# Scores on all 64 partitions of a head: a change to the row count of two products in a one-core decoder layer

## The chip, the cores and the metric

The kernel runs on one core of one Trainium2 chip, as one launch. The metric is device time in microseconds (us), the median of the runs. Three runs of the kernel before gave 5751.36 us as median, from 5746.47 to 5760.46.

## What is computed

A decoder layer in float32, for 8 sequences of 512 tokens with 512 channels. A selective state-space block (1024 inner channels, 16 states), then cross attention with a context of 512 tokens, then a mixture of experts with one shared expert; a layer norm over the sum with its input follows each. The part that the change touches is the attention, 16 heads of 32 channels. Cut to what matters:

```python
qm = split_heads(q @ Wq.T + bq)          # 8 x 16 heads x 512 x 32
km = split_heads(k @ Wk.T + bk)
scores = einsum('bnlh,bnph->bnlp', qm, km) / sqrt(32)
scores = where(mask, scores, -1e8)
attn = softmax(scores, axis=-1)
out = einsum('bnlp,bnph->bnlh', attn, vm)
```

## The kernel before, in words

Three stages follow one another: `layers` (state-space block, attention, shared expert and routing), `experts` (32 experts, each on 640 slots) and `finish` (the last layer norm).

**The layers.** The state-space block works in 16 chunks of 256 tokens, two for each sequence. A chunk has 32 steps (4 pairs of 128 channels, 4 groups of states, 2 halves). In a step VectorE does a product (L441), a scan along time (L445) and a second product (L462), ScalarE the decays before it (L429), and TensorE sums states into `py` (L466). The B and C rows of a step are spread over partitions by copies on SyncE's queue (SP): `bcast`, L373, issued one group of states ahead of their use.

**Units beside the scan.** What comes after the state-space block of sequence b - 1 is cut into some 160 units (`units`), each a TensorE part and what takes its result. The main loop hands them out between the steps of sequence b's two chunks, as many as a written weight allows (`own`, `spent`, `whole`), so TensorE, VectorE and ScalarE take scan and attention work in program order, mixed. The last sequence's units have no scan beside them and run one after another.

**The scores.** Heads go in pairs, 8 pairs to a sequence. Each pair has a buffer `qa` and a buffer `ka` of 128 partitions x 512 tokens, of three each that take turns (`NPB` = 3, L198 to L205). The first head has partitions 0 to 63, the second 64 to 127. Within a head's 64 partitions:

- 0 to 31: queries (`qa`) or keys (`ka`), copied in by `spread` (L717, L718);
- 32: ones in `qa`, the mask's fill value (0 or -1e8) in `ka` (L719);
- 33: minus the largest score of each query in `qa`, put there later by `negate` (L745); ones in `ka`;
- 34 to 63: ones in both, set once at the start, and not read.

`maximum` (L729) takes the product over partitions 0 to 32, 33 rows, for 128 queries by 512 keys, both heads into one tile `ps_s`; VectorE reduces it (L731). `negate` transposes the four columns of maxima of a pair (L738), ScalarE turns the sign (L742), and two copies on SP put the rows into `qa`. `weigh` (L755) then takes the product over partitions 0 to 33, 34 rows, for 128 keys by 512 queries, so that the maximum is taken off within the product; ScalarE takes the exponential (L759). `gather` (L771) multiplies by the values, with a block of ones beside them that gives the sums.

**The order.** In the list of units, step n (n from 0, four to a pair) adds the spread of pair i + 2 when pair i begins, then `maximum` for step n + 6, with `negate` two steps after a pair's last maximum, then `weigh` for step n and `gather` for step n - 1. All copies named go by SP's queue in that order, with `bcast`, weights and the copies of results (L791, L792) between them. A spread waits for the `weigh` that read its buffers three pairs before.

**Setup.** At the start SP issues some 30 small copies of constants; the mask's copy, the weights and the first tokens (`load_x`, L266) stand behind them. GpSimd sets constants at the same time.

Of the kernel before, what the change touches and what calls it, by code (L numbers as in the profile page):

```python
# [16 lines left out]
P = 128  # L17
B, S, D = 8, 512, 512
DC = D // P
# [14 lines left out]
HD = 32  # L34
# [47 lines left out]
def layers(ctx, tc, a, x1d, filld, based, xbuf):  # L82
# [20 lines left out]
    nc = tc.nc  # L103
# [66 lines left out]
    ones = cp.tile([P, P], F32, name="l_ones")  # L170
# [28 lines left out]
    qas, kas = [], []  # L199
    for i in range(NPB):  # L200
        qas.append(cp.tile([P, S], F32, name=f"l_qa{i}"))
        kas.append(cp.tile([P, S], F32, name=f"l_ka{i}"))
        for t in (qas[i], kas[i]):
            for r0 in (HD, 2 * HD + HD):
                nc.gpsimd.memset(t[r0 : r0 + HD], 1.0)  # L205
    va = cp.tile([P, SC, NH // 2, 3 * HD], F32, name="l_va")
    nc.gpsimd.memset(va[:, :, :, HD : 2 * HD], 1.0)

# [435 lines left out]
    def units(b):  # L644
# [66 lines left out]
        def spread(i):  # L711

            n = (b * NH // 2 + i) % NPB
            st[i] = qa, ka = qas[n], kas[n]
            for j in range(2):
                r0, r1 = (i % 2) * 2 * HD + j * HD, j * 2 * HD
                nc.sync.dma_start(qa[r1 : r1 + HD, :], st["qT"][r0 : r0 + HD, i // 2, :])  # L717
                nc.sync.dma_start(ka[r1 : r1 + HD, :], st["kT"][r0 : r0 + HD, i // 2, :])  # L718
                nc.sync.dma_start(ka[r1 + HD : r1 + HD + 1, :], filld[b : b + 1, :])  # L719

        def maximum(i, lt):

            qa, ka = st[i]
            if lt == 0:
                st["mx", i] = p2.tile([P, SC, 2], F32, tag="mx", name="mx")
            ps = pss.tile([P, 2, S], F32, tag="sc", name="ps_s")
            for j in range(2):
                r = slice(j * 2 * HD, j * 2 * HD + HD + 1)
                nc.tensor.matmul(ps[:, j, :], qa[r, lt * P : (lt + 1) * P], ka[r, :], start=True, stop=True)  # L729
            mx = st["mx", i]  # L730
            return lambda: nc.vector.tensor_reduce(mx[:, lt, :].unsqueeze(2), ps, AX.X, ALU.max) and None  # L731
# [17 lines left out]
        def weigh(i, kc):  # L749

            qa, ka = st[i]
            ps = pss.tile([P, 2, S], F32, tag="sc", name="ps_t")
            for j in range(2):
                r = slice(j * 2 * HD, j * 2 * HD + HD + 2)
                nc.tensor.matmul(ps[:, j, :], ka[r, kc * P : (kc + 1) * P], qa[r, :], start=True, stop=True)  # L755

            def exponentials():
                st["eT", i, kc] = eT = p2.tile([P, 2, S], F32, tag="eT", name="eT")
                nc.scalar.activation(eT, ps, AF.Exp)  # L759

            return exponentials
# [116 lines left out]
        for j in range(DC):  # L878
            add(3.4, queries, j, dry=(j == 0))
        add(0, spread, 0)  # L880
        add(0, spread, 1)
        pairs, ahead = NH // 2, SC + 2
        late = []

        def max_at(m):

            if late:
                add(0.4, negate, late.pop(), dry=True)
            if m < pairs * SC:
                add(0.9, maximum, m // SC, m % SC)  # L890
                if m % SC == SC - 1:
                    late.append(m // SC)
# [4 lines left out]
        for n in range(pairs * SC + 4):  # L897
            i, k = n // SC, n % SC
            if k == 0 and i + 2 < pairs:
                add(0, spread, i + 2)  # L900
            max_at(n + ahead)
            if i < pairs:
                add(0.9, weigh, i, k)
            if 0 < n <= pairs * SC:
                add(0.9, gather, (n - 1) // SC, (n - 1) % SC)

            if n > 3 and (n - 3) % (2 * SC) == 0:
                add(0, divide, (n - 3) // (2 * SC) - 1, dry=(n > pairs * SC))
# [78 lines left out]
    for i, (b, t) in enumerate(chunks):  # L987
        nf = {}
        after = chunks[i + 1] if i + 1 < len(chunks) else None
        if t == 0 and b:  # L990
            side, spent = units(b - 1), 0.0

            own = [work(k) for k in range(len(steps))] * 2
            whole = sum(own) + sum(x[0] for x in side)
# [71 lines left out]
    for _, fn, alone in units(B - 1):  # L1066
        do(fn, first=alone)
# [198 lines left out]
def program(tc, a, out):  # L1266
    nc = tc.nc
    with tc.tile_pool(name="dram", bufs=1, space=DRAM) as dram:
        x1d = dram.tile([N, D], F32, name="x1d")
        filld = dram.tile([B, S], F32, name="filld")  # L1270

        based = dram.tile([N + P, D], F32, name="based")
        xbuf = dram.tile([SLOTS, ROW], F32, name="xbuf")
        nc.scalar.preload_act_table_set(LN_EXP)

        with ExitStack() as ctx:
            layers(ctx, tc, a, x1d, filld, based, xbuf)
        with ExitStack() as ctx:
            experts(ctx, tc, a, xbuf, based)
        with ExitStack() as ctx:  # L1280
            finish(ctx, tc, based, out)
# [31 lines left out]
```

## Time and profile before

| what | value |
|---|---|
| median of three runs | 5751.36 us |
| lowest and highest | 5746.47 and 5760.46 us |
| the profiled execution's own time | 5761.86 us |
| its span, first to last instruction | 5760.2 us |
| mean granted TensorE clock | 0.907 |
| TensorE busy, weight loads apart | 5098.1 us |
| VectorE busy | 4111.1 us |
| ScalarE busy | 2554.4 us |
| the layers, up to about | 4080 us |

How to read the lines that the prediction shows. The page gives the busy time of each engine (PE is TensorE's matmul, PEld its weight load, DVE VectorE, ACT ScalarE, POOL GpSimd, SP SyncE's queue), with the span in 40 slices of 144 us below it; a digit of PEclk is the clock that TensorE was granted in that slice, in tenths. A group of instructions has line, engine and operation, what is written from what, the shape, the count; then busy time in all, mean ns of one; then the engine's idle time just before them, and what ended most of it. "33*128 33x512" is a product over 33 rows with 128 stationary columns and 512 streamed ones. A float32 product has two records, and a busy PE is not PE at its peak, as ends are modelled. The table of stretches gives, for each part of the span, its length, each engine's busy time with the count of records, the mean granted clock, the share of the DMA engines and GB/s. A line of waits names who waited, for whom, us in all, times, and the longest.

### The profile page before, as it was taken

How to read it: one execution, taken by the hardware profiler on the slowest of the kernel's cores; microseconds unless marked ns; L12 is line 12 of the kernel's file. 1: busy time of each engine (PE TensorE's matmuls, PEld its weight loads, DVE VectorE, ACT ScalarE, POOL GpSimd, SP SyncE). 2: the span in 40 equal slices, each digit the busy share in tenths (PEclk: the TensorE clock that was granted, in tenths of full speed). 3: DMA queues.
4: the chain of work that ended last, by engine and by line, in shares of the span. 5: the costliest groups of instructions: out<-in, count | busy, mean ns of one | idle time of the engine just before them, and what ended most of it. 6: DMA issues, size and time to landing. Idle time of an engine off the chain costs nothing. (4 is left out here: it accounts for less than half of the span.)

```text
span 5760.2 us, 57381 instructions
## 1 busy us (share of the span) xinstructions
PE 5098.1 (89%) x18984; PEld 2615.0 (45%) x18984; DVE 4111.1 (71%) x5290; ACT 2554.4 (44%) x5347; POOL 514.7 (9%) x424
## 2 busy tenths in 40 slices
PE   5658989888988898989898899889899999999994
PEld 3324344344434433434443443342466666666662
DVE  5998889888889888988988898843444444444443
ACT  4555564554655556455455545523122222222223
POOL 0000001002000100100100020010111111111111
PEclk8779889899889988988988897998999999999997
DMA  7685345335434533533543362431444444444444
GB/s 206 194 230 170 88 120 164 107 112 171 119 107 119 178 95 113 164 105 110 158 131 103 101 192 73 116 123 36 145 119 116 121 115 119 121 122 115 114 122 135
DMA packets 480489, 744.19 MB, mean 129 GB/s; under 512 B 64050, under 2 KB 196666, under 8 KB 480192
## 3 DMA queue, kind: packets, MB, share of 16 engines
q1 hardware_dynamic: 442688, 655.24, 38.0%
q0 software_dynamic: 33280, 76.90, 7.0%
q10 hardware_dynamic: 4224, 8.39, 0.4%
q8 instruction: 150, 2.46, 0.2%
q14 instruction: 147, 1.20, 0.1%
HBM read 491.91 MB, written 148.28 MB: 111 GB/s over the span
## 5 line engine op out<-in xcount | busy, mean ns | idle before, releaser
L429 ACT ACTIVATE l_da<-both,l_aneg 128x256 f32<-128x256 f32 x2048 | 893.6, 499 | 811.0 <-DVE h L445 753.5
L445 DVE TENSOR_TENSOR_SCAN h<-l_da,h 128x1028 f32<-128x1028 f32 x512 | 1170.9, 2292 | 72.7 <-ACT h L435 49.3
L466 PE MATMUL py<-h,l_twice 128*64 128x256 f32 x4096 | 666.4, 438 | 213.6 <-DVE h L462 213.5
L441 DVE TENSOR_TENSOR h<-both,bc 128x1024 f32<-128x1024 f32 x512 | 618.5, 1214 | 167.9 <-PE py L466 108.8
L462 DVE TENSOR_TENSOR h<-h,bc 128x1024 f32<-128x1024 f32 x512 | 622.8, 1218 | 6.0
L466 PEld LDWEIGHTS py<-h,l_twice 128*64 128x64 f32 x4096 | 309.2, 153 | 607.2 <-issue 258.3
L1212 PE MATMUL po<-w,hT 128*128 128x512 f32 x1280 | 575.1, 592 | 0.0
L729 PE MATMUL ps_s<-l_ka,l_qa 33*128 33x512 f32 x1024 | 347.1, 766 | 114.8 <-DVE mx L731 114.4
L1146 PE MATMUL ps_h<-xT,w 128*128 128x320 f32 x1536 | 435.7, 433 | 0.0
L731 DVE TENSOR_REDUCE mx<-ps_s 128x2 f32<-128x1024 f32 x256 | 310.5, 1216 | 115.1 <-PE ps_s L729 114.6
L1167 DVE TENSOR_TENSOR hT<-ps_h,p 128x320 f32<-128x320 f32 x128 | 62.9, 491 | 443.8 <-PE ps_h L1146 443.8
L1217 POOL DMA_INDIRECT based<-y,xe x160 | 251.1, 1569 | 1359.4 <-ACT y L1216 856.6
L1216 ACT ACTIVATE y<-po,xe 128x512 f32<-128x512 f32 x160 | 110.0, 687 | 551.6 <-PE po L1212 542.6
L1146 PEld LDWEIGHTS ps_h<-xT,w 128*128 128x128 f32 x1536 | 292.4, 190 | 131.7 <-issue 15.6
L755 PE MATMUL ps_t<-l_qa,l_ka 34*128 34x512 f32 x1024 | 339.8, 740 | 10.7 <-ACT eT L759 10.3
L771 PE MATMUL po<-eT,l_va 128*64 128x512 f32 x1024 | 322.0, 712 | 16.2 <-ACT raw L783 11.1
L759 ACT ACTIVATE eT<-ps_t 128x1024 f32<-128x1024 f32 x256 | 258.9, 1014 | 174.5 <-PE ps_t L755 174.0
L1212 PEld LDWEIGHTS po<-w,hT 128*128 128x128 f32 x1280 | 231.1, 190 | 231.6 <-issue 224.1
L1146 PE MATMUL ps_h<-t,s 128*128 128x320 f32 x1024 | 286.2, 432 | 0.0
L677 PE MATMUL ps_p<-x2T,wa 128*128 128x512 f32 x512 | 251.1, 642 | 18.2 <-DVE hT L846 16.2
L495 PE MATMUL po<-wm,zs 128*128 128x512 f32 x512 | 245.5, 632 | 22.3 <-DMA wm<-in_out_proj_w 16.8
L297 PE MATMUL ps_x<-xnT,wm 128*128 128x256 f32 x1024 | 255.3, 405 | 4.9 <-ACT dt L395 3.6
(205 smaller groups left out, 6711.3 us busy)
## 6 DMA issues: line engine op xcount, KB each, us to landing
bc<-scr SPq DMA_DIRECT2D x1024, 128.0 KB
w<-in_w SPq DMA_DIRECT2D x96, 1024.0 KB
wm<-in_in_proj_w SPq DMA_DIRECT2D x128, 512.0 KB
xbuf<-zero SPq DMA_DIRECT2D x32, 1362.5 KB
xe<-xbuf SPq DMA_DIRECT2D x32, 1362.5 KB
both<-dt SPq DMA_DIRECT2D x256, 128.0 KB
both<-dtx SPq DMA_DIRECT2D x256, 128.0 KB
wm<-in_out_proj_w SPq DMA_DIRECT2D x64, 512.0 KB
```

The source lines that it names most:

```text
L429: nc.scalar.activation(da[:, n, 1:], dt[:, c % 2, j, :], AF.Exp, scale=aneg[:, c, j, g, m : m + 1])
L441: nc.vector.tensor_tensor(steps, dtx[:, c % 2].unsqueeze(2).to_broadcast([P, 2, NG // 2, T]), bc[0], ALU.mult)
L445: nc.vector.tensor_tensor_scan(flat, da.rearrange("p n t -> p (n t)"), flat, 0.0, ALU.mult, ALU.add)
L462: nc.vector.tensor_tensor(steps, steps, bc[1], ALU.mult)
L466: nc.tensor.matmul(py[j * HP : (j + 1) * HP, c % 2, :], twice, h[:, j * 2 + m, 1:], start=False, stop=(s == (NST // NG - 1, NG // 2 - 1, 1)),)
L729: nc.tensor.matmul(ps[:, j, :], qa[r, lt * P : (lt + 1) * P], ka[r, :], start=True, stop=True)
L731: return lambda: nc.vector.tensor_reduce(mx[:, lt, :].unsqueeze(2), ps, AX.X, ALU.max) and None
L755: nc.tensor.matmul(ps[:, j, :], ka[r, kc * P : (kc + 1) * P], qa[r, :], start=True, stop=True)
L759: nc.scalar.activation(eT, ps, AF.Exp)
L771: nc.tensor.matmul(po[j * 2 * HD : (j + 1) * 2 * HD, :], va[:, kc, i, j * HD : (j + 2) * HD], eT[:, j, :], start=(kc == 0), stop=(kc == SC ...
L1146: nc.tensor.matmul(ps, w[:, n, r * P : (r + 1) * P], x[:, n, :], start=not more and n == 0, stop=n == 1, skip_group_check=more,)
L1212: nc.tensor.matmul(po, got["hT"][:, ic, j * P : (j + 1) * P], got["w2"][:, ic, :], start=(ic == 0), stop=(ic == DC - 1))
```

## The change

The two products go over all 64 partitions of a head, in place of 33 and 34. So that the 30 further rows add nothing, `ka` holds zeros from partition 32 of each head on at the start, and ones in partition 33 alone, which six copies on SP put there at setup[...]. `qa` keeps its ones. Since `maximum` now reads partition 33 too, where `qa` still holds the maxima of three pairs before, `spread` clears that row by one more copy for each head, from a row of zeros of `ka`: two a pair, 128 in all.

```diff
@@ layers, buffers
         for t in (qas[i], kas[i]):
             for r0 in (HD, 2 * HD + HD):
-                nc.gpsimd.memset(t[r0 : r0 + HD], 1.0)
+                nc.gpsimd.memset(t[r0 : r0 + HD], 1.0 if t is qas[i] else 0.0)
+        for r0 in (HD + 1, 2 * HD + HD + 1):
+            nc.sync.dma_start(
+                kas[i][r0 : r0 + 1, :].rearrange("p (c t) -> p c t", c=DC),
+                ones[0:1, :].unsqueeze(1).to_broadcast([1, DC, P]),
+            )
@@ spread
                 nc.sync.dma_start(ka[r1 + HD : r1 + HD + 1, :], filld[b : b + 1, :])
+                nc.sync.dma_start(qa[r1 + HD + 1 : r1 + HD + 2, :], ka[r1 + HD + 2 : r1 + HD + 3, :])
@@ maximum
-                r = slice(j * 2 * HD, j * 2 * HD + HD + 1)
+                r = slice(j * 2 * HD, (j + 1) * 2 * HD)
                 nc.tensor.matmul(ps[:, j, :], qa[r, lt * P : (lt + 1) * P], ka[r, :], start=True, stop=True)
@@ weigh
-                r = slice(j * 2 * HD, j * 2 * HD + HD + 2)
+                r = slice(j * 2 * HD, (j + 1) * 2 * HD)
                 nc.tensor.matmul(ps[:, j, :], ka[r, kc * P : (kc + 1) * P], qa[r, :], start=True, stop=True)
```

## The prediction

> **What bounds the kernel now.** I read the page first, then the busy time of each engine by stretches, then the waits. The page:
>
> ```profile
> span 5760.2 us, 57381 instructions
> ...
> PE 5098.1 (89%) x18984; PEld 2615.0 (45%) x18984; DVE 4111.1 (71%) x5290; ACT 2554.4 (44%) x5347; POOL 514.7 (9%) x424
> ...
> PEclk8779889899889988988988897998999999999997
> ...
> L729 PE MATMUL ps_s<-l_ka,l_qa 33*128 33x512 f32 x1024 | 347.1, 766 | 114.8 <-DVE mx L731 114.4
> L755 PE MATMUL ps_t<-l_qa,l_ka 34*128 34x512 f32 x1024 | 339.8, 740 | 10.7 <-ACT eT L759 10.3
> ```
>
> To be seen: TensorE is busiest, and in the layers (slices 1 to 28) it often has less than its full clock; the two products that change hold 687 us of it. The layers' own bound is read from the scores' stages, the stretch of each batch from its first L729 to its last L771 (the eighth has no scan beside it):
>
> ```profile
> 559.00:799.60 240.60, 214.94 (x894) 91.67 (x892) 212.65 (x205) 142.18 (x286) 0.66 (x5) 0.87 0.37 101
> 1036.00:1278.00 242.00, 216.72 (x892) 91.69 (x892) 212.84 (x205) 142.27 (x286) 1.03 (x7) 0.86 0.36 102
> 1514.60:1754.00 239.40, 213.35 (x892) 90.94 (x892) 212.56 (x205) 142.18 (x286) 0.72 (x5) 0.88 0.36 101
> 1992.00:2240.50 248.50, 219.19 (x894) 91.22 (x892) 212.78 (x206) 143.49 (x288) 1.62 (x6) 0.86 0.35 100
> 2480.40:2729.00 248.60, 221.99 (x892) 93.43 (x892) 212.93 (x205) 142.48 (x286) 1.05 (x4) 0.85 0.34 97
> 2968.50:3217.00 248.50, 222.97 (x892) 93.75 (x892) 212.60 (x205) 143.32 (x287) 1.91 (x5) 0.84 0.35 97
> 3452.00:3701.00 249.00, 225.89 (x854) 88.74 (x852) 205.23 (x188) 136.27 (x270) 0.39 (x3) 0.80 0.34 94
> 3882.80:4000.80 118.00, 117.25 (x417) 34.17 (x418) 45.04 (x41) 44.95 (x54) 0.13 (x1) 0.84 0.14 37
> ```
>
> The columns are us, then busy PE, PEld, DVE, ACT, POOL, then the mean clock. TensorE and VectorE are both near 0.88 in the first seven, so each waits for the other; the eighth is TensorE's alone. The clock is only ever 1.00 or 0.50 in the records, so the time at half speed is 2 x (1 - clock) x length: 63, 68, 57, 70, 75, 80, 100 us, 511 in the seven, and 38 in the eighth. That is the quantity at stake. Why is it slow there?
>
> ```profile
> 3871.00:3887.60 16.60, 16.10 (x46) 6.32 (x44) 3.54 (x4) 2.75 (x4) 0.13 (x1) 1.00 0.28 87
> 3887.60:3925.00 37.40, 37.40 (x87) 10.31 (x86) 10.96 (x10) 7.90 (x9) 0.00 (x0) 0.50 0.06 15
> 3829.70:3856.00 26.30, 26.30 (x62) 11.59 (x61) 5.99 (x15) 4.15 (x8) 0.00 (x0) 1.00 0.24 75
> 3891.00:3897.80 6.80, 6.80 (x18) 2.28 (x16) 3.06 (x4) 1.08 (x2) 0.00 (x0) 0.50 0.01 1
> 842.90:846.30 3.40, 3.40 (x13) 2.31 (x13) 0.54 (x1) 2.85 (x6) 0.00 (x0) 0.50 0.74 209
> 846.30:849.70 3.40, 3.30 (x14) 1.53 (x13) 2.89 (x4) 2.88 (x6) 0.00 (x0) 1.00 0.02 4
> ```
>
> TensorE was 97% busy when the clock fell at 3887.6, and stays at half speed for 37.4 us of unbroken work. What ran was L729 and L755, on 33 and 34 rows for each of two heads, 66 or 68 of 128 rows. Products on 128 rows (3829.7 on, L677) never lose the clock. From the matmuls' records I worked out, for each 3.41 us step before the last one of a stretch, the share of TensorE's time weighted by active rows: the clock falls after a step under about 0.37 and comes back after one over about 0.73. Before the fall at 3887.6 the rows' share was 0.35 and plain occupancy 0.67. Occupancy explains neither: steps at 0.94 to 1.00 stay slow. So the rows are counted.
>
> **What the Trainium skill says.** "TensorE: Matmul & The Clock Gate", Part 1, says that a monitor gates TensorE's clock to half by how busy the array has lately been, over windows of 3413 ns; the trace agrees: two values, and stretches that are multiples of 3.41 us. It doesn't say that rows count; the trace does. Its Part 3 says that a product on few rows takes as long as one on all, the gain being that row groups run at once; here the two heads' records start 7 ns apart. "TensorEngine Tiling (Array Packing)", Tiling Modes, lists row tiles of 32, 64 or 128 rows: 33 and 64 rows need the same 64-row tile, so the pairing should stay. Part 4 of the clock page says that transposes don't count as busy in the same way; the trace disagrees: L832's transposes fill 2.42 of the 3.40 us from 842.9, and the clock rises at their end. This matters doubly, since the identity that they stream is zero in 127 rows of 128: zeros in the stream count.
>
> **The change, part by part.** Products: 1024 records at each line as before, on the same columns. A weight load of 33 rows takes 186 ns (median) and one of 128 rows (L1212) 190, so 64 rows add at most 2048 x 4 ns = 8 us, on a queue that runs under the matmuls: I take 0.
>
> The clock. With 64 in place of 33 and 34 in the rule, on the times of the trace: of 45 slow stretches in the eight stages, 17 don't begin (share before them 0.38 or more), and the others end at the first step over 0.73. Of 549 us at half speed 133 stay: 379 go in the seven stages, 37 in the eighth. What is that worth?
> - Eighth stage: TensorE was busy for all of 37.4 us, so half of it, 18.7; I take 17, as L731's six first reductions (1.22 us each) come to set the pace.
> - Seven stages: VectorE does 212.7 us of work in each (205.2 in the seventh) and is idle for 235 us in all. Upper bound: its idle falls to 7%, some 228 us a stage (220 for the seventh): 12 + 14 + 11 + 20 + 20 + 20 + 29 = 126. Lower bound: the slow stretches get the rate of idle of the fast ones, some 9 to 16%; by stretch that saves 53 us if all slow time goes, 40 for three quarters of it. Two batches of one form tell the slope: 240.7 us with 63 slow (mean of the first three) against 248.5 with 75 (mean of the next three), 0.65 us for each us. I take 75, as scans and sums (L441 to L462) then end last.
>
> VectorE's scan work ends last next; what is left to it is the cover for everything below.
>
> Added copies, 128 on SP's queue (two a pair, the query row set to zero): `l_qa<-nm`, the same 2 KB into one row, issues in 580 ns median, so 1.16 us a pair, 74 us of SP in all. Behind them stand the `bc` copies, the raw sums' copies and the next `nm`. I measured from issue to first use: `bc` in these stages at least 6.6 us, median 20.8; the spread's last copy to its first product 4.1 us at the least, 4.4 in the eighth stage; `nm` to L755 mostly 4 to 16, but 1.5 to 3.6 in about one pair of eight. So only the `nm` copies and the eighth stage can feel it: 14 places by up to 1.16 us, 16 at the most. I take 4, between 0 and 16; a gain has no ground, as a queue only gets longer. The waits are not new:
>
> ```profile
> SPq L717 <- PE ps_t L755: 49.3, 26, 7.5
> DVE h L441 <- DMA bc<-scr: 13.9, 4, 8.5
> ```
>
> The added copy waits for the same L755 as the spread's first one. L729 now reads the row that this copy clears and `nm` later fills: `nm` follows L731, which follows the products, so no wait comes last there.
>
> Setup: six copies of ones on SP at 18.9 us, ahead of the mask's and of x's: 6 x 0.43 to 0.63 us (issues at L125 and L146) = 2.6 to 3.8, on the path, as the first scan waits for x: 3. Memsets only change value: 0.
>
> Sum: -17 - 75 + 4 + 3 = -85. Against the profiled execution's 5761.9 us: 5677. It ran 10.5 us above the median of the runs, 5751.4; from the median I forecast 5667.
>
> **Rivals.**
> 1. VectorE's order takes over: the clock rises, but the seven stages give 5 to 25 us, as their idle is waits on ScalarE and on order. For: it is 88% busy. Against: the slope of 0.65. Time: about -25, 5726.
> 2. The clock doesn't move (the monitor looks at values, or at row groups of 32). For: the trace has no product whose extra rows are zeros through and through. Against: the transposes; and by groups, 33 rows would count as 64 already. Time: +4 + 3, 5758, up to 5770.
> 3. Slower: the heads lose their pairing. Now two records that start 7 ns apart share 0.43 us until the next two (L729 at 3882.75, 3883.29, 3883.72). If 64 rows a head don't run at once, each of 1024 such steps costs 0.43 us more, 440 us: 55 in the eighth stage, in full, and 385 in the seven, at the slope of 0.65 some 250. Less the gain of 85 that is +220: 5971. It decides once some 280 of the 1024 steps (85 / (0.43 x 0.7)) come apart. Against: 33 rows already need a 64-row tile.
> 4. SP stands: the added copy reads `l_ka`, which the copies just before it write in other rows. If it has to wait until they land (3.4 us for the mask's copy, issued at 18.95, used at 22.35), a pair costs SP 2 x (3.4 + 0.6) = 8 us, 4 over the cover of 4 at two pairs of eight and in the eighth stage: 24 places, 96 us, which takes the gain: about 5760. Against: the rows don't meet.
>
> **How the numbers follow.** Likeliest, 0.70: 5667, between -143 (126 + 18.7, copies at 3) and -45 (40 + 17, copies at 12), so 5608 to 5706. Rival 1, 0.12; rival 2, 0.10; rival 3, 0.05; rival 4, 0.03. The range 5605 to 5745 holds the likeliest and rival 1, 0.82. A measurement tells 0.3%, 17 us, from no change. Faster: 0.70 and most of rival 1, less a rest, 0.78; within: that rest and most of rivals 2 and 4, 0.13; slower: rival 3 and the end of rival 2, 0.09.
>
> **What would show it.** Right: from 3887 on the eighth stage stays at 1.00 and takes about 100 us for 118; the seven stages show 0.95 or more and some 228 to 238 us; PEclk in slices 5 to 26 rises to 9; L729 and L755 still pair, with means nearer 640 ns; x load some 3 us later. Wrong: the same clock beside 64 rows (rival 2); a higher clock at the same stage lengths (rival 1); products of 64 rows that no longer start together (rival 3); SP waiting at the new line for its own copies (rival 4).

## The result and the profile after

The changed kernel takes **5662.84 us** (median of 4 runs, 5654.88 to 5674.74), the kernel before, run beside it, 5753.27 us (4 runs, 5746.47 to 5760.46). The ratio is 0.9844, 95% interval [0.9823, 0.9866]: 90 us less. The forecast was 5667. The profiled execution took 5660.41 us, 2 us under its median, where that of before was 10 us over its own; so the two spans differ by 101.5 us, and the sums below are made against that. The page after:

```profile
span 5658.7 us, 57578 instructions
...
PE 4933.6 (87%) x18984; PEld 2576.2 (46%) x18984; DVE 4107.3 (73%) x5290; ACT 2548.5 (45%) x5347; POOL 525.2 (9%) x424
...
PEclk8778999999999999999999999999999999999997
...
L735 PE MATMUL ps_s<-l_ka,l_qa 64*128 64x512 f32 x1024 | 316.9, 698 | 140.8 <-DVE mx L737 140.6
L761 PE MATMUL ps_t<-l_qa,l_ka 64*128 64x512 f32 x1024 | 303.3, 655 | 12.9 <-ACT eT L765 9.0
```

The two products have the same 1024 records each on nearly twice the rows, and are shorter: 698 ns for 766 and 655 for 740. TensorE's busy time fell by 165 us with no instruction taken away, and the clock stands at 9 from slice 5 on, where it used to fall to 8 and 7 through the layers. TensorE now also waits longer for the reduction (140.6 us for 114.4). The stages of the eight batches, in the columns used for the kernel before:

```profile
562.20:794.30 232.10, 200.36 (x892) 87.72 (x892) 212.15 (x205) 142.81 (x287) 2.54 (x5) 0.93 0.39 110
1034.10:1267.90 233.80, 196.60 (x892) 86.35 (x892) 212.17 (x205) 141.90 (x286) 2.54 (x5) 0.96 0.36 104
1507.20:1739.20 232.00, 200.01 (x894) 87.40 (x892) 212.15 (x205) 141.72 (x287) 2.54 (x5) 0.94 0.37 105
1978.30:2210.20 231.90, 198.69 (x892) 86.16 (x892) 212.17 (x205) 141.66 (x286) 2.61 (x7) 0.95 0.38 107
2449.30:2680.10 230.80, 199.43 (x892) 87.10 (x892) 212.15 (x205) 141.25 (x286) 0.76 (x4) 0.94 0.37 105
2917.00:3149.00 232.00, 199.34 (x894) 87.36 (x892) 212.16 (x205) 141.94 (x286) 2.54 (x5) 0.94 0.37 104
3384.80:3609.70 224.90, 193.46 (x852) 80.86 (x852) 203.69 (x188) 135.01 (x270) 0.36 (x3) 0.94 0.36 103
3797.70:3899.80 102.10, 100.80 (x419) 30.50 (x418) 45.06 (x41) 44.89 (x54) 0.13 (x1) 1.00 0.17 43
```

By the starts of their first and last records the seven stages sum to 1617.5 us for 1716.7, and the eighth takes 102.1 for 118.1: 99.2 and 16.0 us less. VectorE's work in a stage is what it was (212.2 us), and the stage is shorter around it: over the seven it is 91% busy for 86%. The first scan starts 3.7 us later, and the stretches between the stages are 10.9 us longer; what lies behind the eighth stage is as long as it was. Together that makes the 101.5 to within a us.

By the clock's records the stages now hold 184 us at half speed (outside them it is 534 us for 523), none of it in the eighth, where before held 549. The kind of stretch has changed too. Of 45 stretches with a mean of 12 us there are now 42 with a mean of 4.4, each of one or two steps of 3.41 us. (A step is one window of the clock's records; its row share is the part of it in which TensorE streams, weighted by the active rows out of 128.) Two of them, each with the step ahead of it (busy time by stretches, after):

```profile
2017.50:2020.90 3.40, 0.96 (x6) 0.30 (x4) 3.40 (x7) 3.40 (x9) 0.00 (x0) 1.00 0.10 36
2020.90:2024.30 3.40, 3.40 (x10) 0.92 (x9) 3.40 (x7) 3.09 (x6) 0.10 (x1) 0.50 0.35 100
2089.20:2092.60 3.40, 1.06 (x6) 0.30 (x4) 2.99 (x3) 2.74 (x6) 0.00 (x0) 1.00 0.09 21
2092.60:2096.00 3.40, 3.40 (x14) 0.82 (x10) 1.22 (x1) 0.35 (x1) 0.00 (x0) 0.50 0.24 58
```

TensorE was busy for 0.96 and 1.06 of 3.40 us ahead of the fall, while VectorE was busy for 3.40 and 2.99: these are real pauses. One busy step at half speed brings the clock back, as the Trainium skill says in "TensorE: Matmul & The Clock Gate", Part 1, of one busy window of about 3.4 us; 30 of the 42 stretches are a single step, the other 12 two. Over all 42, counted from the matmuls' records, the row share ahead of the fall is 0.39 or less and lies within 0.02 of plain occupancy in 38 (within 0.08 in the other four), and the step that ends the stretch has 0.80 or more. So the forecast's rule fits the new trace with its lower bound within 0.02, and the kind of fall that it was to remove, one that outlasts busy steps, is gone. What VectorE waits for in all, before and after:

```profile
DVE mx L731 <- PE ps_s L729: 114.6, 60, 24.8
DVE h L441 <- PE py L466: 108.8, 54, 5.3
```

```profile
DVE mx L737 <- PE ps_s L735: 81.0, 34, 25.0
DVE h L446 <- PE py L471: 58.3, 25, 7.8
```

The columns are us in all, times, longest. These two waits of VectorE for TensorE are 84 us shorter, of 223. The second is the scan's own sum (`collect`), which the change doesn't touch: the clock is everyone's on that engine.

### The profile page after: what moved, and what is told of

Read it like the earlier page. It is cut to its first block, busy times and chain, and to the rows that moved or that the text cites. A ratio compares the mean times of both kernels' runs of the same rounds, so it can differ in the third digit from the quotient of the medians.

```text
span 5658.7 us, 57578 instructions
## 1 busy us (share of the span) xinstructions
PE 4933.6 (87%) x18984; PEld 2576.2 (46%) x18984; DVE 4107.3 (73%) x5290; ACT 2548.5 (45%) x5347; POOL 525.2 (9%) x424
## 5 line engine op out<-in xcount | busy, mean ns | idle before, releaser
L471 PE MATMUL py<-h,l_twice 128*64 128x256 f32 x4096 | 632.4, 421 | 225.9 <-DVE h L467 225.7
L735 PE MATMUL ps_s<-l_ka,l_qa 64*128 64x512 f32 x1024 | 316.9, 698 | 140.8 <-DVE mx L737 140.6
L761 PE MATMUL ps_t<-l_qa,l_ka 64*128 64x512 f32 x1024 | 303.3, 655 | 12.9 <-ACT eT L765 9.0
L777 PE MATMUL po<-eT,l_va 128*64 128x512 f32 x1024 | 278.8, 623 | 21.2 <-ACT raw L789 18.1
L302 PE MATMUL ps_z<-xnT,wm 128*128 128x256 f32 x1024 | 241.6, 389 | 12.7 <-DMA wm<-in_in_proj_w 12.7
```

What stands on the lines that cost most here:

```text
L471: nc.tensor.matmul(py[j * HP : (j + 1) * HP, c % 2, :], twice, h[:, j * 2 + m, 1:], start=False, stop=(s == (NST // NG - 1, NG // 2 - 1, 1)),)
L777: nc.tensor.matmul(po[j * 2 * HD : (j + 1) * 2 * HD, :], va[:, kc, i, j * HD : (j + 2) * HD], eT[:, j, :], start=(kc == 0), stop=(kc == SC ...
```

## The experiments

The theory: the monitor of the clock counts active rows, whatever they hold; with 64 rows a head the products keep the clock up, and the time comes from that alone, shared between TensorE's half-speed stretches and VectorE's waits for them. The rivals: values count, or rows in blocks of 32; the gain comes from the new layout or order rather than the rows; VectorE's work alone is what ends the stages, before or after; the clock follows plain occupancy, or active cells (rows times columns), and not rows. Each ratio is to the kernel before on the same chip.

**The copies without the rows** (e1_copies_only): the whole change, but the products on 33 and 34 rows.

```diff
-                r = slice(j * 2 * HD, (j + 1) * 2 * HD)
+                r = slice(j * 2 * HD, j * 2 * HD + HD + 1)
...
-                r = slice(j * 2 * HD, (j + 1) * 2 * HD)
+                r = slice(j * 2 * HD, j * 2 * HD + HD + 2)
```

> The change without its rows: zeros, ones, the six copies at setup and the 128 clearing copies stay, the products go over 33 and 34 rows as before. Theory (the row count raises the clock): the clock stays at 0.907 and only the costs are left, 3 to 4 us at setup and up to 16 for SP, so about +7 us against the kernel before, 5760, between +2 and +20. Rival (the contents or the order of the copies bring the gain, the rows don't): about -90 us, clock 0.935.

Measured: 5771.34 us against 5741.52, ratio 1.0048 [1.0031, 1.0065], 28 us more (18 to 37). Two stages and the eighth:

```profile
561.70:810.40 248.70, 224.92 (x893) 94.36 (x892) 212.84 (x205) 144.00 (x287) 1.08 (x5) 0.84 0.36 103
1050.50:1291.50 241.00, 218.51 (x894) 92.14 (x892) 212.87 (x205) 142.36 (x286) 1.06 (x5) 0.86 0.36 100
3901.50:4017.80 116.30, 115.29 (x419) 33.93 (x418) 45.04 (x41) 44.99 (x54) 0.13 (x1) 0.87 0.15 37
```

The clock is back at 0.84 to 0.87 and the stages at their old lengths: the rows make the gain, not the copies or the contents. But the extras cost more than the forecast's 4 + 3. In this profiled execution, 15.5 us longer than that of before, the scores' stages are together 9 us shorter and the stretches between them 23 us longer, and outside the stages the clock is at half speed for 559 us instead of 523: the extra time lies where the scores' products don't run. The last experiment takes its cause up.

**One product at a time** (e2_weigh_rows, e3_max_rows): 64 rows in `weigh` alone with 33 in `maximum`, then 64 in `maximum` alone with 34 in `weigh`; each is one half of the diff above.

> 64 rows in the second product alone, 33 in the one for the maximum; all else as changed. Theory: the rule on the trace of before leaves about 250 us of 549 at half speed in the scores' stages in place of 130, so part of the gain, some -60 us (-35 to -80), and in the eighth stage a short fall where maxima run alone. Rival (only the products' sum of data counts): no gain, +7 us.

> 64 rows in the product for the maximum alone, 34 in the second; all else as changed. Theory: the rule leaves about 190 us at half speed, so -75 us (-45 to -90), no fall in the eighth stage where maxima run alone. The two halves don't add up to the whole, as each alone lifts mixed steps over the threshold. Rival (the second product alone matters, as ScalarE waits on it): nearly nothing, +7 to -15 us.

Measured: 5690.6 us, 0.9903 [0.9882, 0.9925], and 5697.94 us, 0.9908 [0.9886, 0.9931]: the halves are worth the same. Against the copies-only kernel on the same chip that is 81 and 73 us, where both together (the next kernel) give 115: either half alone takes two thirds. In each the eighth stage has no half-speed time and takes 102.1 us; e2's:

```profile
3826.40:3928.50 102.10, 100.83 (x419) 30.49 (x418) 45.04 (x41) 44.85 (x54) 0.13 (x1) 1.00 0.17 43
```

The rule says why. The lowest row share of a step there is 0.41 in e2 and 0.53 in e3, over 0.37, so the clock doesn't fall; in the kernel before it fell after 0.36. There it also stayed down: in work that alternates the two products, 66 and 68 rows of 128 give at most a share of 0.53, which can't reach 0.73. I had expected a short fall in e2, and there was none.

**All zeros** (e4_both_zero): the query rows past the ones hold zeros as well, so both operands are zero there.

```diff
-                nc.gpsimd.memset(t[r0 : r0 + HD], 1.0 if t is qas[i] else 0.0)
+                nc.gpsimd.memset(t[r0 : r0 + HD], 0.0)
+        for r0 in (HD, 3 * HD):
+            nc.gpsimd.memset(qas[i][r0 : r0 + 1], 1.0)
```

> As changed, but the query buffer holds zeros too in rows 34 to 63, so that both operands of the further rows are zero in both products. Theory (the count of rows in the instruction is what the monitor sees): the same as the changed kernel, about -90 us, clock 0.935 to 0.937. Rival (the monitor sees work on values, and ones against zeros were enough): the clock falls back toward 0.907 and the gain with it, -40 us or less.

Measured: 5656.51 us, 0.9847 [0.9826, 0.9869], clock 0.937, the same as after. The values in the added rows don't count.

**Another layout, without copies** (e5_memset_64, e6_memset_34): `nm` goes to partition 32 and the mask's row to 33 of each head. The ones of `ka` and the clearing of the query row then begin at partition 32, GpSimd sets both there, and SP gets no copy more. e5 has 64 rows in both products, e6 has 34.

```diff
-        for r0 in (HD + 1, 2 * HD + HD + 1):
-            nc.sync.dma_start(
-                kas[i][r0 : r0 + 1, :].rearrange("p (c t) -> p c t", c=DC),
-                ones[0:1, :].unsqueeze(1).to_broadcast([1, DC, P]),
-            )
+        for r0 in (HD, 2 * HD + HD):
+            nc.gpsimd.memset(kas[i][r0 : r0 + 1], 1.0)
...
-                nc.sync.dma_start(ka[r1 + HD : r1 + HD + 1, :], filld[b : b + 1, :])
-                nc.sync.dma_start(qa[r1 + HD + 1 : r1 + HD + 2, :], ka[r1 + HD + 2 : r1 + HD + 3, :])
+                nc.sync.dma_start(ka[r1 + HD + 1 : r1 + HD + 2, :], filld[b : b + 1, :])
+                nc.gpsimd.memset(qa[r1 + HD : r1 + HD + 1, :], 0.0)
...
-                    r0 = j * 2 * HD + HD + 1
+                    r0 = j * 2 * HD + HD
```

> 64 rows in both products without any added copy: the row for the maxima moves to partition 32 of a head and the mask's row to 33, so that GpSimd sets the ones at setup and clears the maxima's row in the spread; SP's queue is that of the kernel before. Theory (rows raise the clock, the added copies cost what the run of the copies alone showed, 28 us): -100 to -120 us against the kernel before. Rival (the copies' cost arises only beside a falling clock and is near nothing once the clock stays up): the same as the changed kernel, -88 us.

> The same layout and GpSimd's clearing, with 34 rows in both products: the contents of the changed kernel with neither its rows nor its copies. Theory: no difference from the kernel before, within 10 us, clock 0.905 to 0.91, so that the 28 us of the copies alone come from SP. Rival (the contents, or the maxima's product waiting for its cleared row, cost them): +15 to +30 us.

Measured: e5 5648.87 us, 0.9824 [0.9795, 0.9852], the lowest ratio of those that do the whole computation (e11 below ties with it), though its interval overlaps that of the change. e6 5760.1 us, 1.0016 [1.0000, 1.0032]. One layout with one order of work, and 111 us between 34 rows and 64: of the pairs here, the one in which nothing but the rows differs and nothing is added to SP.

**Rows between** (e9_rows_40, e10_rows_48): the layout of e5, and 40 or 48 rows in both products.

```diff
-                r = slice(j * 2 * HD, (j + 1) * 2 * HD)
+                r = slice(j * 2 * HD, j * 2 * HD + 40)
```

> The layout that GpSimd clears, with 40 rows in both products (34 and 64 in the two runs before it). Theory (rows are counted one by one, with a fall under a share of 0.37 and a return over 0.73): the rule on the trace of before leaves 355 us of 549 at half speed in the scores' stages, against 130 with 64 rows; at the 0.25 us for each us that 64 rows gave, -49 us, between -20 and -75. Rival (rows count by blocks, or full tiles alone): as with 34 rows, within 15 us of the kernel before.

> The same with 48 rows. Theory: the rule leaves 242 us, so -77 us, between -50 and -100, between the runs with 40 and with 64 rows. Rival (blocks of rows): equal to the one with 34 or the one with 64.

Measured: 5714.75 us, 0.9930 [0.9904, 0.9956], and 5679.11 us, 0.9876 [0.9850, 0.9901]. The row of `maximum`'s product on the four pages, 34, 40, 48 and 64 rows, with the clock line of the first and last:

```profile
PEclk8779889789988978988998897998899999999997
...
L732 PE MATMUL ps_s<-l_ka,l_qa 34*128 34x512 f32 x1024 | 358.0, 784 | 99.6 <-DVE mx L734 99.3
```

```profile
L732 PE MATMUL ps_s<-l_ka,l_qa 40*128 40x512 f32 x1024 | 341.6, 750 | 109.3 <-DVE mx L734 109.2
```

```profile
L732 PE MATMUL ps_s<-l_ka,l_qa 48*128 48x512 f32 x1024 | 317.0, 699 | 131.8 <-DVE mx L734 131.7
```

```profile
PEclk8779999999999999999999999999999999999997
...
L732 PE MATMUL ps_s<-l_ka,l_qa 64*128 64x512 f32 x1024 | 316.5, 695 | 141.4 <-DVE mx L734 141.2
```

| rows a head | clock, median of the runs | us to before, by the ratio | eighth stage, us |
|---|---|---|---|
| 34 | 0.905 | +9 | 126.5 |
| 40 | 0.914 | -40 | 110.2 |
| 48 | 0.928 | -71 | 103.5 |
| 64 | 0.938 | -101 | 103.8 |

Each step up in rows raises the clock and lowers the time; the intervals of 48 and 64 rows just touch. The eighth stage is that of the profiled execution, which with 34 rows was 30 us over its median. 34, 40, 48 and 64 rows are all over 32 and not over 64, so a count in blocks of 32 would have given one time; that falls. The eighth stage again follows the rule: at 40 rows the clock falls twice, after steps of 0.36, and 13.6 us at half speed stay; at 48 rows the lowest step has 0.44, and there is no fall.

Two more rivals can be settled from the traces that are there. Counting every step of the eight stages in all 14 traces (a record of 512 columns taken as 0.43 us at full clock, the spacing of their starts, and as double at half clock), there are 5758 steps at full clock, 627 of them followed by a fall. The bound of 0.37 on the row share puts 39 of the 5758 on the wrong side; plain occupancy, at the bound that suits it best, 188; active cells, rows times columns, 241. Of the 1512 steps at half clock, the bound of 0.73 puts 66 on the wrong side, and the other two at their best 540 and 411. So the clock goes by rows, as near as these records tell.

**Half of the reduction** (e7_half_max on the changed kernel, e8_half_max_before on the one before): the maxima are taken over the first 256 of the 512 keys alone. All else runs, so VectorE loses some 16 us of work a stage and TensorE none.

```diff
-            return lambda: nc.vector.tensor_reduce(mx[:, lt, :].unsqueeze(2), ps, AX.X, ALU.max) and None
+            return lambda: nc.vector.tensor_reduce(mx[:, lt, :].unsqueeze(2), ps[:, :, 0 : S // 2], AX.X, ALU.max) and None
```

> As changed, but VectorE's reduction of the scores takes the first 256 of 512 keys alone; the maximum over the other half is left out. It frees VectorE of some 256 x 0.55 = 140 us, about 125 of them beside the scan. Theory (VectorE's work ends last in the scores' stages once the clock stays up): most of that shows, -90 us or more against the changed kernel, so -170 to -200 against the kernel before. Rival (the stages are set by order and by ScalarE): -30 us or less against the changed kernel, about -120.

> The kernel before with the same half of the reduction left out. Theory (there TensorE at half speed and VectorE hold each other up): less comes out than with the changed rows, -30 to -70 us, as TensorE's share of the bound stays. Rival (VectorE alone was the bound before too): the same -90 us or more as with the changed rows.

Measured: e7 5615.84 us, 0.9773 [0.9746, 0.9800], which is 41 us less than the change gives; e8 5749.57 us, 0.9994 [0.9974, 1.0013], nothing. First and eighth stage of e7, then of e8:

```profile
563.70:787.30 223.60, 195.80 (x892) 85.83 (x892) 196.20 (x205) 140.25 (x285) 1.49 (x4) 0.95 0.40 114
3749.70:3850.80 101.10, 100.57 (x417) 30.67 (x418) 28.18 (x41) 44.89 (x54) 0.13 (x1) 1.00 0.17 43
```

```profile
558.50:796.30 237.80, 216.40 (x892) 91.35 (x892) 196.66 (x205) 139.93 (x284) 1.11 (x4) 0.86 0.36 102
3824.50:3962.50 138.00, 137.74 (x419) 39.42 (x418) 28.18 (x41) 45.19 (x54) 0.13 (x1) 0.72 0.12 31
```

Before, VectorE's work was not what held the whole: with 113 us less of it in the seven stages the kernel gained nothing over 22 runs (between 15 us less and 7 more). How that comes about inside isn't shown. The profiled execution of e8 took 5722.48 us, 27 under the median; its seven stages are 53 us shorter than those of before, and its eighth, at a clock of 0.72, 20 us longer, so one execution can gain much in the stages. After, the same cut takes 41 us from the seven stages, 37% of what was freed, and the median shows it. VectorE is now a bound, but not the only one: TensorE, busy for 196 of 223.6 us, is close behind. I had expected 90 us or more from e7, and 30 to 70 from e8; both were wrong.

**More rows elsewhere** (e11_dt_rows): e5, and the step sizes' product (L384 of the kernel before) over 64 rows instead of 32, its weights padded with rows of zeros.

```diff
-    w_dt = const("w_dt", [RANK, DI], a["dt_proj_w"])
+    w_dt = cp.tile([2 * RANK, DI], F32, name="l_w_dt")
+    nc.gpsimd.memset(w_dt[RANK : 2 * RANK], 0.0)
+    nc.sync.dma_start(w_dt[0:RANK], a["dt_proj_w"])
...
-                ps[:, i, :], w_dt[:, c * P : (c + 1) * P], f["xd"][0:RANK, :], start=True, stop=True
+                ps[:, i, :], w_dt[:, c * P : (c + 1) * P], f["xd"][0 : 2 * RANK, :], start=True, stop=True
```

> The layout that GpSimd clears with 64 rows in both products, and the step-size product (32 rows, 256 records in a row of four each) over 64 rows too, with zeros in its weights' further rows. Theory: the records are few, 0.4 us in a step of 3.4 at most, so only steps near a threshold tip: -5 us against the same kernel without, between -15 and +5. Rival (this product's few rows begin the falls that are left): -20 us or more.

Measured: 5658.03 us, 0.9824 [0.9797, 0.9852], clock 0.937: the same as e5. So the few rows of this product don't make the half-speed time that is left, which fits the pauses in the stretches above.

**The 128 copies alone** (e12_row_copies): the kernel before and nothing but the clearing copies. In it they write ones into a row that `nm` overwrites before it counts.

```diff
                 nc.sync.dma_start(ka[r1 + HD : r1 + HD + 1, :], filld[b : b + 1, :])
+                nc.sync.dma_start(qa[r1 + HD + 1 : r1 + HD + 2, :], ka[r1 + HD + 2 : r1 + HD + 3, :])
```

> The kernel before with nothing but spread's 128 added copies on SP (one row of ones of ka into query row 33, which nm overwrites before it counts); 33 and 34 rows in the products, no setup copies, the same values in every row that the products read. The first theory says that the cost of +28 us (18 to 37) of the copies-only kernel lies in these copies on SP's queue: +15 to +28 us here, 5757 to 5780 by the clock of 0.90. The prediction's own estimate was +4 (0 to 16). The rival says that the cost lies in the setup's six copies (+3.7 us at the first scan) and in the zeros that stand in the rows: 0 to +5 us here.

Measured: 5762.59 us against 5757.93, ratio 1.0004 [0.9990, 1.0018], so 2 us, between -6 and +10. The copies' own row (duration in ns at least, median and at most), here and in the changed kernel:

```profile
L720 SPq DMA_DIRECT2D l_qa<-l_ka x128: 497/519/1297, 508.7 to 3994.3; - x128
L720 SPq EVENT_SEMAPHORE  x1: 17/17/17, 3925.3 to 3925.3; - x1
```

```profile
L725 SPq DMA_DIRECT2D l_qa<-l_ka x128: 497/519/977, 512.3 to 3870.6; - x128
L725 SPq EVENT_SEMAPHORE  x1: 17/17/17, 3818.6 to 3818.6; - x1
```

SP issues each in 519 ns and stood at that line once, for 17 ns. My theory that the 28 us of e1 lay in these copies falls. Contents like those of the change can give part of it at most: e6, which has them in another order of rows and without copies, costs 0 to 18. What is left to e1 alone is the setup's six copies, seen as 3.7 us at the first scan. Those six were not run by themselves, so some 15 us of e1 stay unexplained; its profiled execution has them between the scores' stages.

## Why the prediction was right, step by step

- **The quantity at stake, and the rule.** Right in kind: rows count, near one by one, zeros count, and the bounds of 0.37 and 0.73 hold in the trace after, the lower one to within 0.02. The half-speed time left was mis-sized: 133 us forecast, 184 measured. What failed is "17 don't begin", read as 28 that stay. Stretches did end at their first busy step or one later, much as said; but they begin nearly as often as before (42 for 45). All 42 follow a step in which TensorE streamed for 0.42 of the time or less; of the old 45, by the same count, 31 did. So a faster TensorE runs out of work more often and pauses, for VectorE in the two stretches shown, and a pause lowers the clock as well as few rows do. The forecast took the times of the old trace, which hold none of these new pauses.
- **Eighth stage: -17.** Measured -16.0, at a clock of 1.00 throughout; the reductions set the first pace, with a stop of 0.49 us after eight records; the same stop stood in the kernel before, ahead of the fall of its clock (timeline of TensorE, first before, then after):

```profile
3882.75 1.99 PE L729 MATMUL ps_s<-l_ka,l_qa 33*128 33x512 f32 x8
3885.23 1.13 PE L729 MATMUL ps_s<-l_ka,l_qa 33*128 33x512 f32 x4 [0.49 <-DVE mx L731]
```

```profile
3797.70 1.99 PE L735 MATMUL ps_s<-l_ka,l_qa 64*128 64x512 f32 x8
3800.18 2.26 PE L735 MATMUL ps_s<-l_ka,l_qa 64*128 64x512 f32 x8 [0.49 <-DVE mx L737]
```

- **Seven stages: -75.** Mis-sized: -99.2 between the profiles, from less half-speed time removed than forecast (328 us for 379). So a us at half speed was worth 0.30 us, not 0.20, and not the 0.65 that was read as a slope. In the experiments it is 0.28 in e2 against e1 (81 us for 287) and 0.35 in e3 (73 for 212). The seven came within 3 to 6 us of the upper bound of 228 (220 for the last). My reserve, that the scans' own order would hold them back further, was too large.
- **Added copies: +4.** Right: 2 us (-6 to +10) where they were run alone, and no wait at the new line.
- **Setup: +3.** 3.7 us at the first scan. That e1 as a whole costs 28 isn't accounted for by this term and the copies. Under the raised clock little of it shows: the change and e5, which has no such copies, lie 12 us apart, with overlapping intervals.
- **"VectorE's scan work ends last next."** Right in part: a cut of VectorE's work in these stages (the reductions, not the scans) shows 37% after and nothing before.
- **The sum.** -85 forecast, -90 by the medians and -101.5 between the two profiled executions. The closeness is in part luck: the seven stages gave 24 us more than forecast, from less half-speed time at a higher worth, and 11 us of that was given back between the stages, which the forecast put at nothing; and the profiled execution of before was one of the longer ones.
- **Readings and sums that don't hold.** The seven times at half speed as listed add to 513 us, not 511 (the clock's records: 512). VectorE was 0.82 to 0.89 busy in the seven stages of before, 0.86 in all, not near 0.88 throughout. The far end of the likeliest range, 126 + 18.7 with copies at 3, is 142 and not 143, and both ends leave the setup out. In rival 4 the eighth stage is counted twice: 14 and 8 places make 22, and 88 us. None of it moves the forecast.
- **Readings of the Trainium skill.** That few rows take as long as all is stated in the last section of the clock page, "Why this matters for your kernels", not in its Part 3; the runs agree (1.99 us for eight records on 33 and on 64 rows). That the trace disagrees with Part 4 isn't shown: L832's transposes have two records each, 213 ns apart at half clock for 128 columns, the rate of the products (853 ns for 512), and no record tells whether the transposing mode, of which Part 4 speaks, was on. What the trace shows is that these transposes count for the clock; that zeros count is shown by e4.

The rivals: VectorE's order (5 to 25 us from the seven stages) falls by the 99 us there. The clock that doesn't move falls by the page, by e4 and by the rows between. The lost pairing falls by the timelines above: eight records take 1.99 us on 64 rows as on 33; with "TensorEngine Tiling (Array Packing)", Tiling Modes, in the Trainium skill, 33 to 64 rows need the same tile, and the trace agrees. SP standing at its own copies falls by L725's 17 ns. Of the signs named ahead, one was missed narrowly: the seven clocks are 0.93 to 0.96, where 0.95 or more was to be seen.

## What to carry to other kernels

Where TensorE's clock is low beside a busy TensorE, weight its busy time by active rows, step by step: here, work that filled the time but not the rows kept the clock down for up to 44 us on end in the kernel before, and filling the unused rows with zeros cost no matmul time. Before pricing the engine that "ends last next", cut its work and see, before and after: TensorE and VectorE were 0.89 and 0.86 busy, and the cut showed that VectorE didn't hold the time before and held part of it after. Price a raised clock also by the new pauses that it makes.

## What the runs showed that was not expected

- **The length of the slow stretch varies widely.** With 33 or 34 rows the eighth stage has one unbroken stretch at half speed in each of five profiled executions: 31 us (e1), 37 (before), 51 (e6), 55 (e12) and 78 (e8), with the stage from 116.3 to 138.0 us long. By the rule it ends only when a step happens to pass 0.73, and their steps mostly lie between 0.4 and 0.75. e8, with less work on VectorE, has the longest; whether the cut makes it so isn't shown by one execution.
- **Most of the gain is there at 48 rows.** 48 rows a head give 71 of the 101 us and most of the rise of the clock (0.928 for 0.938); `maximum`'s records average 699 and 695 ns.
- **Chips differ.** The kernel before has medians of 5741.5 to 5757.9 us on the chips used here, 16 us apart, so each kernel is held only against the runs of before on its own chip.
